# A gated recurrence over 512 steps: the columns of its three PSUM banks regrouped to 192, 128 and 64

## The chip, the cores and the metric

The kernel runs on one core of one Trainium2 chip. The metric is the device time in microseconds (us) of one launch; the time before is the median of three runs.

## The reference

Eight sequences (batch B = 8) of T = 512 steps with 512 features go through a gated recurrent cell with 512 units, and the cell's output is added to its input. All arithmetic is float32.

```python
def step(h, x_t):
    fused = jax.nn.sigmoid(jnp.concatenate([x_t, h], axis=-1) @ w_W + w_b)
    hidden_state, output_state = jnp.split(fused, 2, axis=-1)          # r, z
    memory_state = x_t @ wx_W + wx_b + hidden_state * (h @ wh_W + wh_b)
    h_new = output_state * h + (1.0 - output_state) * jnp.tanh(memory_state)
    return (h_new, h_new)
_, hs = jax.lax.scan(step, h0, jnp.swapaxes(x, 0, 1))
out = x + jnp.swapaxes(hs, 0, 1)
```

In the kernel's names, r is the gate on the hidden product, z the gate that keeps the old state, hh the product h @ wh_W with its bias, and x the product x_t @ wx_W with its bias. Every step needs the state of the step before.

## The kernel before

**Layout.** The state is kept with units on partitions, in four tiles of 128 units, k = 0 to 3. Half A is k = 0 and 1 (tiles `hTA`), half B is k = 2 and 3 (`hTB`). A matmul takes the state as the loaded weights (128 partitions, 32 columns: four steps of eight sequences, of which the rows of the current step are filled and the others are zero) and streams weight columns against it. Its output lies on 32 PSUM partitions. Index j = 0 to 3 names the four such strips, each with its own 128 of the 512 units, so that one (bank, k) is four matmuls, one for each strip. The strips can run side by side on TensorE. Each float32 matmul appears in the trace as two records.

**Banks.** Four steps make a group, g. Each group has three PSUM banks of 128 columns, in two sets for even and odd groups: R holds r of both halves, G holds hh and z of half A, H holds z and hh of half B. ScalarE first copies the x-side products into a bank (`spread`, L248 at the copy), and the matmuls of the steps then accumulate onto them.

**One step on TensorE.** The order is written out: `ORDER = "R0 R1 G0 G1 R2 R3 G2 G3 H0 H1 H2 H3"`, four matmuls for each word, 48 in all, so R0 needs the first tile of the new state and R2 the third. After them come seven matmuls of 192 columns for the x-side of a later group (`products`, tiles `xp`), from step 5 on until the last ten steps, for which none are left. The strip at which a step starts is turned by seven each time, so that the three spare places rotate. All matmuls go through one helper and have line L188.

**One step on VectorE and ScalarE.** VectorE takes the sums back to units-on-partitions by 32x32 transposes, and does the gating by scans (`tensor_tensor_scan`: multiply by one operand, add the other), one for each k. ScalarE does the sigmoids and the tanh. All its activations have line L216.

- `turn_r(hf)`: transpose of r into `tr` (L377), sigmoid into `md0`.
- `turn_h(hf)`: transpose of hh into `md1` (L395).
- `turn_z(hf)`: transpose of z into `tz` (L377), sigmoid of the negative into `hd0`. Its transpose is made to wait for the sigmoid of r by a manual dependency.
- `memory(hf)`: two scans `m` from `md0` and `md1` (L357), each followed by a tanh on ScalarE into a slot of the state tile.
- `update(hf)`: two scans from `hd0` and the state tile into the next state tile (L357), one for each k.

The order of these calls is the order on both engines:

```python
turn_r(0); turn_r(1); turn_h(0); turn_z(0); memory(0); update(0)
turn_h(1); turn_z(1); memory(1); update(1)
```

After that follow, in each step, two copies of the new state into another slot (ScalarE), one transpose of an x-side block for the next group (`turn_x`, L252), in some steps copies and sums for the x-side, three tiny memsets (L497), and two additions of input and state on GpSimd (L499) into the output tile. VectorE, ScalarE and GpSimd each work in the order written.

**Loads.** SP loads the weights at the start (`wx`, `wgr`, `whh`) and then one chunk of 16 steps of x at a time, and stores the output by chunks.

Of the kernel before, what the change touches and what calls it, by code (L numbers as in the profile page):

```python
# [7 lines left out]
F32 = mybir.dt.float32  # L8
BF16 = mybir.dt.bfloat16
AF = mybir.ActivationFunctionType  # L10
ALU = mybir.AluOpType
PSUM = bass.MemoryType.PSUM

P = 128
NQ = 4
GS = 4
B = 8
HU = 64
# [5 lines left out]
LAST = 4  # L24
SYNC = mybir.DependencyInfo(mybir.DependencyClass.Sync, mybir.DependencyReason.DATA)

ORDER = "R0 R1 G0 G1 R2 R3 G2 G3 H0 H1 H2 H3"

FIRST = "Q0 x Q1 x Q2 x Q3 H0 H1 H2 H3"

BANKS = ("R", "G", "H")

HALF = 192

AL, BE = (0, slice(64, 256)), (0, slice(256, 448))
GA, DE = (1, slice(64, 256)), (1, slice(256, 448))

XP = {"G": slice(0, 128), "R": slice(128, 256), "X": slice(256, 384), "H": slice(384, 512)}


@with_exitstack
def tile_cond_rnn_residual(
# [2 lines left out]
    x: bass.AP,  # L45
    xh: bass.AP,
    wx_d: bass.AP,
    wgr_d: bass.AP,
    whh_d: bass.AP,
    wh3_d: bass.AP,  # L50
    bias_d: bass.AP,
    out: bass.AP,
    TC: int,
# [28 lines left out]
    nc = tc.nc  # L82
    NCH = x.shape[0]
    T = NCH * TC
    NG = T // GS

    const = ctx.enter_context(tc.tile_pool(name="const", bufs=1))
    xin_p = ctx.enter_context(tc.tile_pool(name="xin", bufs=4))
    out_p = ctx.enter_context(tc.tile_pool(name="outp", bufs=3))
    work = ctx.enter_context(tc.tile_pool(name="work", bufs=4))  # L90
    psum = ctx.enter_context(tc.tile_pool(name="psum", bufs=1, space=PSUM))
# [31 lines left out]
    wx = const.tile([P, NQ, NQ, 384], F32, name="wx")  # L123
    for k in range(NQ):
        nc.sync.dma_start(out=wx[:, k], in_=wx_d[k])

    wgr = const.tile([P, NQ, NQ, 256], F32, name="wgr")
    for k in range(NQ):
        nc.sync.dma_start(out=wgr[:, k], in_=wgr_d[k])
    whh = const.tile([P, NQ, NQ, 128], F32, name="whh")  # L130
    nc.sync.dma_start(out=whh[:, :3], in_=whh_d)
    nc.sync.dma_start(out=whh[:, 3], in_=wh3_d)

    def wh(bank, k, j):
        return whh[:, k, j] if bank == "H" else wgr[:, k, j, {"G": slice(0, 128), "R": slice(128, 256), "Q": slice(0, 256)}[bank]]

    load_x(0, 1)

# [6 lines left out]
    NH = 2 * GS  # L145
# [29 lines left out]
    def state(hf, i, slot=2):  # L175

        s = i % GS
        return hT[hf][i % NH][:, B * s : B * s + B, :, slot]

    ctx.enter_context(tc.manual_schedule())  # L180
    banks = [
        {n: psum.tile([P, 128], F32, name=f"{n}{q}") for n in BANKS}
        for q in range(2)
    ]
    xps = [psum.tile([P, 512], F32, name=f"xp{q}") for q in range(2)]
# [1 line left out]
    def mm(out_, lhsT, rhs, start=False):  # L187
        nc.tensor.matmul(  # L188
            out_, lhsT, rhs, start=start, stop=False, skip_group_check=True
        )  # L190


    for t_ in list(banks[0].values()) + list(banks[1].values()):
        mm(t_, none[:, :128], none, start=True)
    def warm():

        mm(xps[1], zeros[:, :128], zeros)
# [17 lines left out]
    def act(key, out_, in_, func, **kw):  # L215
        inst = nc.scalar.activation(out_, in_, func, **kw).ins  # L216
        if key in written:
            tc.declare_no_dep(inst, written[key], reason="ordered through VectorE")
        written[key] = inst
        return inst  # L220
# [17 lines left out]
    def late(g):  # L238

        if g == 0:  # L240
            return xps[0][:, 256:512]
        return even if g % 2 == 0 else odd[g // 2 % 2]

    def spread(g, names):

        for n in names:
            src = late(g)[:, 128:256] if n == "H" else xps[g % 2][:, XP[n]]
            nc.scalar.copy(banks[g % 2][n], src)  # L248

    def turn_x(g, e):  # L250

        nc.vector.transpose(  # L252
            md1[e // 2][g % 2][:, :, e % 2, 1], late(g)[:, 32 * e : 32 * e + 32]
        )

    def reg(r):
        return xps[r[0]][:, r[1]]
# [61 lines left out]
    first = {g: prefill(g) for g in (1, 2, 3)}  # L319
    weight_sum(0)  # L320
    weight_sum(2)
    spread(0, "RGH")
    for e in range(NQ):
        turn_x(0, e)

    pool_done = {}
    for i in range(T):
# [7 lines left out]

        for n in (ORDER if i else FIRST).split():
            if n == "x":
                take(first[1], 1)
                continue
            bank, k = n[0], int(n[1])  # L340
            hs = hT[k // 2][i % NH][:, :, k % 2, 2]
            for j in range(NQ):
                j = (j + turn[0]) % NQ
                to = xps[0][:, :256] if bank == "Q" else ps[bank]
                mm(to[32 * j : 32 * j + 32, :], hs, wh(bank, k, j))
        if i < 5:
            take(first[(i + 3) // 2], 2)
# [3 lines left out]

        rows = slice(B * s, B * s + B)

        def scans(hf, out_, d0, d1):

            for c_ in (slice(0, 1), slice(1, 2)):
                nc.vector.tensor_tensor_scan(  # L357
                    *[t_[:, :, c_].rearrange("p n c s -> p (n c s)") for t_ in (out_, d0, d1)],
                    0.0,
                    ALU.mult,  # L360
                    ALU.add,
                )
                yield c_

        if i:
            pg, pr = ps["G"], ps["R"]
        else:
            pg, pr = (xps[0][:, XP[n]] for n in "GR")
        raw = {
            "h": (pg[:, :HU], ps["H"][:, HU:]),  # L370
            "z": (pg[:, HU:], ps["H"][:, :HU]),
            "r": (pr[:, :HU], pr[:, HU:]),
        }

        def turned(n, hf):
            t_ = work.tile([P, 2, 32], F32, tag=f"t{n}{hf}", name=f"t{n}{hf}_{i}")
            inst = nc.vector.transpose(t_.rearrange("p c n -> p (c n)"), raw[n][hf]).ins  # L377
            return t_[:, :, rows], inst
# [1 line left out]
        r_done = [None, None]  # L380

        def turn_r(hf):
            tr, inst = turned("r", hf)

            if hf == 1 and i + 1 - NH in pool_done:
                tc.add_manual_dep(inst, pool_done[i + 1 - NH].name, SYNC)
            r_done[hf] = act(
                ("r", hf, g % 2, s),
                md0[hf][g % 2][:, rows, :, 1].rearrange("p n c -> p c n"),
                tr,  # L390
                AF.Sigmoid,
            )

        def turn_h(hf):
            nc.vector.transpose(  # L395
                md1[hf][g % 2][:, :, :, 0].rearrange("p n c -> p c n"), raw["h"][hf]
            )

        def turn_z(hf):
            tz, inst = turned("z", hf)  # L400

            tc.add_manual_dep(inst, r_done[hf].name, SYNC)
            act(
                ("zc", hf, i % 2),
                hd0[hf][i % 2][:, :, :, 2].rearrange("p n c -> p c n"),
                tz,
                AF.Sigmoid,
                scale=-1.0,
            )

        def memory(hf):

            m = work.tile([P, 2, B, 2], F32, tag=f"m{hf}", name=f"m{hf}_{i}").rearrange("p c n s -> p n c s")
            for c_ in scans(hf, m, md0[hf][g % 2][:, rows], md1[hf][g % 2][:, rows]):
                act(("n", hf, c_.start, i % NH), state(hf, i, 1)[:, :, c_], m[:, :, c_, 1], AF.Tanh)

        def update(hf):
            s1 = (i + 1) % GS
            new = hT[hf][(i + 1) % NH][:, B * s1 : B * s1 + B]
            for _ in scans(hf, new, hd0[hf][i % 2], hT[hf][i % NH][:, rows]):  # L420
                pass

        turn_r(0)
        turn_r(1)
        turn_h(0)
        turn_z(0)
        memory(0)
        update(0)
        if i == 0:

            seed(2)
        if i == T - 1:
# [3 lines left out]
                state(0, T),  # L436
                ALU.add,
            )
        turn_h(1)
        turn_z(1)  # L440
        memory(1)
        update(1)
        for hf in range(2):
            act(("h", hf, (i + 1) % NH), state(hf, i + 1, 0), state(hf, i + 1), AF.Copy)
        if i < 3:
# [3 lines left out]
        nxt, two = o + 1 < NG // 2, o + 2 < NG // 2  # L449
        if i == 0:  # L450
            nc.scalar.copy(odd[0], xps[1][:, 256:512])
        if g + 1 < NG:
            turn_x(g + 1, s)
        if i == 0:
            spread(1, "R")
        if u == 0:
            spread(2 * o + 1, "G")
            if o and nxt:
                nc.scalar.copy(reg(GA), reg(BE))
        elif u == 1:  # L460
            spread(2 * o + 1, "H")
        elif u == 2 and o == 0:
            seed(3)
            nc.scalar.copy(even, xps[0][:, 256:512])
        elif u == 2 and nxt:
            last = odd[(o + 1) % 2][:, :HALF]
            nc.vector.tensor_tensor(last, reg(GA), both, ALU.add)
        elif u == 3 and nxt:
            if o:
                nc.vector.tensor_tensor(even[:, :HALF], reg(BE), both, ALU.add)  # L470
            spread(2 * o + 2, "R")
        elif u == 4 and nxt:
            if o == 0:
                nc.scalar.copy(odd[1], xps[1][:, 256:512])
            spread(2 * o + 2, "G")
            if two:
                nc.scalar.copy(reg(AL), bias[:, AL[1]])
                x_sum(o + 2, 0)
        elif u == 5 and nxt:
            spread(2 * o + 2, "H")  # L480
            if two:
                nc.scalar.copy(reg(DE), step_bias)
                x_sum(o + 2, 1)
        elif u == 6 and two:
            nc.scalar.copy(reg(BE), reg(AL))
            x_sum(o + 2, 2)
        elif u == 7 and nxt:
            spread(2 * o + 3, "R")
            if two:
                nc.scalar.copy(both, reg(DE))  # L490
                x_sum(o + 2, 3)
# [104 lines left out]
```

## Time and profile before

| | |
|---|---|
| Time, three runs | 1681.29 us median (1680.15 to 1682.52) |
| Profiled execution, own time | 1682.46 us |
| Its span, first to last instruction | 1679.9 us |
| Granted TensorE clock, mean | 0.999 |
| TensorE matmul busy | 1668.8 us, 99% of the span |
| VectorE busy | 1144.5 us, 68% |
| ScalarE busy | 947.4 us, 56% |
| GpSimd busy | 303.5 us, 18% |
| DMA moved | 31.37 MB, mean 19 GB/s |

The profile is of one execution. Busy shares count time in which at least one instruction of the engine is recorded; matmul records overlap, since they are pipelined. A line of the timeline gives start and duration in us, engine, line, operation, output and inputs with shapes, how many instructions are merged, and in brackets the idle time of the engine before it with what ended that. The view rounds to 10 ns; the trace's records, from which single steps are read, are in ns. "Seen" means that the waiting engine starts, some time after the record of the producer ended.

### The profile page before, as it was taken

How to read it: one execution, taken by the hardware profiler on the slowest of the kernel's cores; microseconds unless marked ns; L12 is line 12 of the kernel's file. 1: busy time of each engine (PE TensorE's matmuls, PEld its weight loads, DVE VectorE, ACT ScalarE, POOL GpSimd, SP SyncE). 2: the span in 40 equal slices, each digit the busy share in tenths (PEclk: the TensorE clock that was granted, in tenths of full speed). 3: DMA queues.
4: the chain of work that ended last, by engine and by line, in shares of the span. 5: the costliest groups of instructions: out<-in, count | busy, mean ns of one | idle time of the engine just before them, and what ended most of it. 6: DMA issues, size and time to landing. Idle time of an engine off the chain costs nothing.

```text
span 1679.9 us, 129621 instructions
## 1 busy us (share of the span) xinstructions
PE 1668.8 (99%) x56206; PEld 1645.4 (98%) x56206; DVE 1144.5 (68%) x9387; ACT 947.4 (56%) x5822; POOL 303.5 (18%) x1281
## 2 busy tenths in 40 slices
PE   8999999999999999999999999999999999999998
PEld 5999999999999999999999999999999999999997
DVE  6766666666666666666666666666666666666666
ACT  3555555555555555555555555555555555555554
POOL 1111111111111111111111111111111111111111
PEclk9999999999999999999999999999999999999999
DMA  4000000000000000000000000000000000000000
GB/s 178 17 5 17 18 18 17 17 5 18 17 18 18 5 17 18 17 17 5 18 18 17 18 15 7 18 17 17 17 5 18 17 18 17 5 18 12 11 11 10
DMA packets 11523, 31.37 MB, mean 19 GB/s; under 512 B 1220, under 2 KB 1732, under 8 KB 10952
## 3 DMA queue, kind: packets, MB, share of 16 engines
q1 hardware_dynamic: 10800, 22.94, 3.9%
q8 instruction: 439, 7.19, 1.7%
q14 instruction: 132, 1.08, 0.2%
q10 hardware_dynamic: 152, 0.16, 0.0%
HBM read 14.70 MB, written 8.39 MB: 14 GB/s over the span
## 4 chain that ended last, share of the span: by engine, by line
PE 99%; DVE 1%; DMA 0%; ACT 0%; issue 0%
PE R L188 27%; PE G L188 26%; PE H L188 26%; PE xp L188 19%; DMA rows<-in_bias_dram 0%; DVE md1A L395 0%; DVE hTA L357 0%; ACT hd0A L216 0%; DVE tz L377 0%; ACT hTA L216 0%; DVE bias L203 0%; DVE rows L120 0%; ACT hTB L216 0%; DVE hTB L357 0%; ACT hd0B L216 0%
## 5 line engine op out<-in xcount | busy, mean ns | idle before, releaser
L188 PE MATMUL R<-wgr,hTA 128*32 128x128 f32 x8176 | 431.5, 275 | 2.4 <-DVE hTA L357 2.2
L188 PE MATMUL G<-wgr,hTA 128*32 128x128 f32 x8176 | 411.9, 273 | 0.0
L377 DVE STREAM_TRANSPOSE tr<-R 128x64 f32<-128x64 f32 x1022 | 194.4, 228 | 286.9 <-PE R L188 286.8
L188 PE MATMUL R<-wgr,hTB 128*32 128x128 f32 x8176 | 385.9, 275 | 0.0
L499 POOL TENSOR_TENSOR ot<-xin,hTB 128x16 f32<-128x16 f32 x503 | 126.6, 252 | 1331.5 <-DVE hTB L357 1323.4
L188 PE MATMUL H<-whh,hTB 128*32 128x128 f32 x8192 | 366.4, 273 | 0.0
L188 PE MATMUL H<-whh,hTA 128*32 128x128 f32 x8192 | 366.2, 273 | 0.0
L188 PE MATMUL G<-wgr,hTB 128*32 128x128 f32 x8176 | 365.5, 273 | 0.0
L188 PEld LDWEIGHTS G<-wgr,hTA 128*32 128x32 f32 x8176 | 334.5, 122 | 0.2
L188 PEld LDWEIGHTS R<-wgr,hTA 128*32 128x32 f32 x8176 | 301.2, 123 | 9.0 <-DVE hTA L357 5.5
L188 PEld LDWEIGHTS H<-whh,hTB 128*32 128x32 f32 x8192 | 289.0, 122 | 0.1
L188 PEld LDWEIGHTS H<-whh,hTA 128*32 128x32 f32 x8192 | 289.0, 122 | 0.1
L188 PEld LDWEIGHTS G<-wgr,hTB 128*32 128x32 f32 x8176 | 288.6, 122 | 0.0
L216 ACT ACTIVATE hd0B<-tz 128x16 f32<-128x16 f32 x512 | 116.5, 228 | 279.4 <-DVE tz L377 279.3
L188 PEld LDWEIGHTS R<-wgr,hTB 128*32 128x32 f32 x8176 | 255.2, 123 | 2.2 <-DVE hTB L357 0.5
L216 ACT ACTIVATE md0A<-tr 128x16 f32<-128x16 f32 x512 | 112.0, 219 | 237.5 <-DVE tr L377 237.4
L188 PE MATMUL xp<-tw,sx 128*32 128x192 f32 x2976 | 229.3, 326 | 0.0
L357 DVE TENSOR_TENSOR_SCAN hTB<-hd0B,hTB 128x24 f32<-128x24 f32 x1024 | 158.0, 196 | 104.6 <-ACT hTB L216 104.4
L357 DVE TENSOR_TENSOR_SCAN hTA<-hd0A,hTA 128x24 f32<-128x24 f32 x1024 | 157.7, 195 | 103.2 <-ACT hTA L216 103.2
L188 PE MATMUL xp<-wx,xin 128*32 128x192 f32 (+1 forms) x2048 | 178.2, 331 | 0.4 <-issue 0.4
L216 ACT ACTIVATE hd0A<-tz 128x16 f32<-128x16 f32 x512 | 115.7, 226 | 111.1 <-DVE tz L377 111.1
L216 ACT ACTIVATE hTB<-hTB 128x16 f32<-128x16 f32 x512 | 120.4, 235 | 79.6 <-DVE hTB L357 70.9
(90 smaller groups left out, 2408.9 us busy)
## 6 DMA issues: line engine op xcount, KB each, us to landing
xin<-in_x_dram SPq DMA_DIRECT2D x31, 256.0 KB, 3.5
out_dram<-ot SPq DMA_DIRECT2D x31, 256.0 KB, 2.2
wx<-in_wx_dram SPq DMA_DIRECT2D x4, 768.0 KB, 7.0
wgr<-in_wgr_dram SPq DMA_DIRECT2D x4, 512.0 KB, 9.7
whh<-in_whh_dram SPq DMA_DIRECT2D x1, 768.0 KB
whh<-in_wh_dram SPq DMA_DIRECT2D x1, 256.0 KB, 10.9
out_dram<-ot SPq DMA_DIRECT2D x1, 192.0 KB, 1.8
head<-in_xh_dram ACTq DMA_DIRECT2D x1, 144.0 KB, 5.0
```

The source lines that it names most:

```text
L188: nc.tensor.matmul(out_, lhsT, rhs, start=start, stop=False, skip_group_check=True)
L216: inst = nc.scalar.activation(out_, in_, func, **kw).ins
L357: nc.vector.tensor_tensor_scan(*[t_[:, :, c_].rearrange("p n c s -> p (n c s)") for t_ in (out_, d0, d1)], 0.0, ALU.mult, ALU.add,)
L377: inst = nc.vector.transpose(t_.rearrange("p c n -> p (c n)"), raw[n][hf]).ins
L499: return engine.tensor_tensor(ot[:, t, 2 * hf : 2 * hf + 2, :].rearrange("p c n -> p n c"), x_of(c, slice(2 * hf, 2 * hf + 2), t, 1).rearr ...
```

## The change

The columns are dealt to the banks anew. Bank A holds hh, z and r of half A (192 columns), bank B holds r and hh of half B (128), bank C holds z of half B (64). The order on TensorE becomes `A0 B0 A1 A2 A3 B1 B2 B3 C0 C1 C2 C3`. On VectorE and ScalarE, r of half B is turned after the memory scans of half A; the two updates of half A are set apart, with turn_r(1) before the first and turn_h(1) and turn_z(1) between them. turn_z(0) keeps its wait for the sigmoid of r; turn_z(1) loses it, and the second update of half A takes it. The wait for GpSimd moves from turn_r(1) to turn_h(0). The x-side tile is laid out to match (192 columns for A, then X, C and B), turn_x runs one step earlier and reads some blocks from PSUM, and the weight tiles are regrouped (`wa` 192 columns, `wb` 192). The number of matmuls, transposes, scans and activations of a step stays the same.

```diff
-ORDER = "R0 R1 G0 G1 R2 R3 G2 G3 H0 H1 H2 H3"
+ORDER = "A0 B0 A1 A2 A3 B1 B2 B3 C0 C1 C2 C3"
-FIRST = "Q0 x Q1 x Q2 x Q3 H0 H1 H2 H3"
+FIRST = "A0 x A1 x A2 x A3 B0 B1 B2 B3 C0 C1 C2 C3"
-BANKS = ("R", "G", "H")
+BANKS = {"A": 192, "B": 128, "C": 64}
...
-XP = {"G": slice(0, 128), "R": slice(128, 256), "X": slice(256, 384), "H": slice(384, 512)}
+XP = {"A": slice(0, 192), "X": slice(192, 320), "C": slice(320, 384), "B": slice(384, 512)}
...
     def wh(bank, k, j):
-        return whh[:, k, j] if bank == "H" else wgr[:, k, j, {"G": slice(0, 128), "R": slice(128, 256), "Q": slice(0, 256)}[bank]]
+        return wa[:, k, j] if bank == "A" else wb[:, k, j, {"C": slice(0, 64), "B": slice(64, 192)}[bank]]
...
     def turn_x(g, e):
-        nc.vector.transpose(
-            md1[e // 2][g % 2][:, :, e % 2, 1], late(g)[:, 32 * e : 32 * e + 32]
-        )
+        c0 = XP["X"].start + 32 * e
+        nc.vector.transpose(md1[e // 2][g % 2][:, :, e % 2, 1], part(g, c0, c0 + 32))
...
         raw = {
-            "h": (pg[:, :HU], ps["H"][:, HU:]),
-            "z": (pg[:, HU:], ps["H"][:, :HU]),
-            "r": (pr[:, :HU], pr[:, HU:]),
+            "h": (pa[:, :HU], ps["B"][:, HU:]),
+            "z": (pa[:, HU : 2 * HU], ps["C"]),
+            "r": (pa[:, 2 * HU :], ps["B"][:, :HU]),
         }
...
         def turn_r(hf):
-            tr, inst = turned("r", hf)
-            if hf == 1 and i + 1 - NH in pool_done:
-                tc.add_manual_dep(inst, pool_done[i + 1 - NH].name, SYNC)
+            tr, _ = turned("r", hf)
...
         def turn_h(hf):
-            nc.vector.transpose(
+            inst = nc.vector.transpose(
                 md1[hf][g % 2][:, :, :, 0].rearrange("p n c -> p c n"), raw["h"][hf]
-            )
+            ).ins
+            if hf == 0 and i + 1 - NH in pool_done:
+                tc.add_manual_dep(inst, pool_done[i + 1 - NH].name, SYNC)
         def turn_z(hf):
             tz, inst = turned("z", hf)
-            tc.add_manual_dep(inst, r_done[hf].name, SYNC)
+            if hf == 0:
+                tc.add_manual_dep(inst, r_done[0].name, SYNC)
...
         turn_r(0)
-        turn_r(1)
         turn_h(0)
         turn_z(0)
-        memory(0)
-        update(0)
+        memory(0, 0)
+        memory(0, 1)
+        turn_r(1)
+        update(0, 0)
+        turn_h(1)
+        turn_z(1)
+        tc.add_manual_dep(update(0, 1), r_done[1].name, SYNC)
...
-        turn_h(1)
-        turn_z(1)
-        memory(1)
-        update(1)
+        memory(1, 0)
+        memory(1, 1)
+        update(1, 0)
+        update(1, 1)
...
-        if g + 1 < NG:
-            turn_x(g + 1, s)
+        ahead = 2 * o + (1 if u < 3 else 2 if u < 7 else 3)
+        if ahead < NG:
+            turn_x(ahead, (u + 1) % GS)
...
-            spread(2 * o + 1, "G")
+            spread(2 * o + 1, "B")
...
-            spread(2 * o + 1, "H")
+            spread(2 * o + 1, "C")
...
-            spread(2 * o + 2, "R")
+            spread(2 * o + 2, "A")
```

Here `memory(hf, q)` and `update(hf, q)` do one of the two scans (and, for memory, its tanh) that `memory(hf)` and `update(hf)` did in a loop.

More of the change, by code (lines that the diff above doesn't have):

```diff
@@ L47, in tile_cond_rnn_residual @@
     wx_d: bass.AP,
-    wgr_d: bass.AP,
-    whh_d: bass.AP,
-    wh3_d: bass.AP,
+    wa_d: bass.AP,
+    wb_d: bass.AP,
+    wb3_d: bass.AP,
     bias_d: bass.AP,
@@ L125, in tile_cond_rnn_residual @@
         nc.sync.dma_start(out=wx[:, k], in_=wx_d[k])
-    wgr = const.tile([P, NQ, NQ, 256], F32, name="wgr")
+    wa = const.tile([P, NQ, NQ, 192], F32, name="wa")
     for k in range(NQ):
[L129 to L132, printed above, removed]
+        nc.sync.dma_start(out=wa[:, k], in_=wa_d[k])
+    wb = const.tile([P, NQ, NQ, 192], F32, name="wb")
+    nc.sync.dma_start(out=wb[:, :3], in_=wb_d)
+    nc.sync.dma_start(out=wb[:, 3], in_=wb3_d)
     def wh(bank, k, j):
-        return whh[:, k, j] if bank == "H" else wgr[:, k, j, {"G": slice(0, 128), "R": slice(128, 256), "Q": slice(0, 256)}[bank]]
+        return wa[:, k, j] if bank == "A" else wb[:, k, j, {"C": slice(0, 64), "B": slice(64, 192)}[bank]]
     load_x(0, 1)
@@ L181, in tile_cond_rnn_residual @@
     banks = [
-        {n: psum.tile([P, 128], F32, name=f"{n}{q}") for n in BANKS}
+        {n: psum.tile([P, w], F32, name=f"{n}{q}") for n, w in BANKS.items()}
         for q in range(2)
@@ L193, in tile_cond_rnn_residual @@
     for t_ in list(banks[0].values()) + list(banks[1].values()):
-        mm(t_, none[:, :128], none, start=True)
+        mm(t_, none, none[:, :1].broadcast_to([P, t_.shape[1]]), start=True)
     def warm():
@@ L242, in late, with part @@
         return even if g % 2 == 0 else odd[g // 2 % 2]
+    def part(g, c0, c1):
+        return late(g)[:, c0 - 256 : c1 - 256] if c0 >= 256 else xps[g % 2][:, c0:c1]
     def spread(g, names):
         for n in names:
-            src = late(g)[:, 128:256] if n == "H" else xps[g % 2][:, XP[n]]
-            nc.scalar.copy(banks[g % 2][n], src)
+            nc.scalar.copy(banks[g % 2][n], part(g, XP[n].start, XP[n].stop))
     def turn_x(g, e):
-        nc.vector.transpose(
-            md1[e // 2][g % 2][:, :, e % 2, 1], late(g)[:, 32 * e : 32 * e + 32]
-        )
+        c0 = XP["X"].start + 32 * e
+        nc.vector.transpose(md1[e // 2][g % 2][:, :, e % 2, 1], part(g, c0, c0 + 32))
     def reg(r):
@@ L321, in tile_cond_rnn_residual @@
     weight_sum(2)
-    spread(0, "RGH")
+    spread(0, "BCA")
     for e in range(NQ):
@@ L343, in tile_cond_rnn_residual @@
                 j = (j + turn[0]) % NQ
-                to = xps[0][:, :256] if bank == "Q" else ps[bank]
+                to = ps[bank] if i or bank != "A" else xps[0][:, XP["A"]]
                 mm(to[32 * j : 32 * j + 32, :], hs, wh(bank, k, j))
@@ L352, in tile_cond_rnn_residual, with scan @@
         rows = slice(B * s, B * s + B)
[L354 to L361, printed above, removed]
-                )
[L363 to L368, printed above, removed]
+        def scan(c_, out_, d0, d1):
+            return nc.vector.tensor_tensor_scan(
+                *[t_[:, :, c_].rearrange("p n c s -> p (n c s)") for t_ in (out_, d0, d1)],
+                0.0,
+                ALU.mult,
+                ALU.add,
+            ).ins
+        pa = ps["A"] if i else xps[0][:, XP["A"]]
         raw = {
-            "h": (pg[:, :HU], ps["H"][:, HU:]),
-            "z": (pg[:, HU:], ps["H"][:, :HU]),
-            "r": (pr[:, :HU], pr[:, HU:]),
+            "h": (pa[:, :HU], ps["B"][:, HU:]),
+            "z": (pa[:, HU : 2 * HU], ps["C"]),
+            "r": (pa[:, 2 * HU :], ps["B"][:, :HU]),
         }
@@ L394, in turn_h @@
         def turn_h(hf):
-            nc.vector.transpose(
+            inst = nc.vector.transpose(
                 md1[hf][g % 2][:, :, :, 0].rearrange("p n c -> p c n"), raw["h"][hf]
-            )
+            ).ins
+            if hf == 0 and i + 1 - NH in pool_done:
+                tc.add_manual_dep(inst, pool_done[i + 1 - NH].name, SYNC)
         def turn_z(hf):
             tz, inst = turned("z", hf)
-            tc.add_manual_dep(inst, r_done[hf].name, SYNC)
+            if hf == 0:
+                tc.add_manual_dep(inst, r_done[0].name, SYNC)
             act(
@@ L409, in turn_z, with memory, update @@
             )
[L411 to L417, printed above, removed]
+        ms = [
+            work.tile([P, 2, B, 2], F32, tag=f"m{hf}", name=f"m{hf}_{i}").rearrange("p c n s -> p n c s")
+            for hf in range(2)
+        ]
+        def memory(hf, q):
+            c_ = slice(q, q + 1)
+            scan(c_, ms[hf], md0[hf][g % 2][:, rows], md1[hf][g % 2][:, rows])
+            act(("n", hf, q, i % NH), state(hf, i, 1)[:, :, c_], ms[hf][:, :, c_, 1], AF.Tanh)
+        def update(hf, q):
             s1 = (i + 1) % GS
             new = hT[hf][(i + 1) % NH][:, B * s1 : B * s1 + B]
-            for _ in scans(hf, new, hd0[hf][i % 2], hT[hf][i % NH][:, rows]):
-                pass
+            return scan(slice(q, q + 1), new, hd0[hf][i % 2], hT[hf][i % NH][:, rows])
         turn_r(0)
-        turn_r(1)
         turn_h(0)
         turn_z(0)
-        memory(0)
-        update(0)
+        memory(0, 0)
[5 more added lines that the diff above has]
+        tc.add_manual_dep(update(0, 1), r_done[1].name, SYNC)
         if i == 0:
@@ L451, in tile_cond_rnn_residual @@
             nc.scalar.copy(odd[0], xps[1][:, 256:512])
-        if g + 1 < NG:
-            turn_x(g + 1, s)
-        if i == 0:
-            spread(1, "R")
+            spread(1, "A")
+            turn_x(1, 0)
+        ahead = 2 * o + (1 if u < 3 else 2 if u < 7 else 3)
+        if ahead < NG:
+            turn_x(ahead, (u + 1) % GS)
         if u == 0:
-            spread(2 * o + 1, "G")
+            spread(2 * o + 1, "B")
             if o and nxt:
@@ L474, in tile_cond_rnn_residual @@
                 nc.scalar.copy(odd[1], xps[1][:, 256:512])
-            spread(2 * o + 2, "G")
+            spread(2 * o + 2, "B")
             if two:
@@ L479, in tile_cond_rnn_residual @@
         elif u == 5 and nxt:
-            spread(2 * o + 2, "H")
+            spread(2 * o + 2, "C")
             if two:
@@ L487, in tile_cond_rnn_residual @@
         elif u == 7 and nxt:
-            spread(2 * o + 3, "R")
+            spread(2 * o + 3, "A")
             if two:
@@ L551 @@
     w, wxm, whm = f["L0_cond_w_W"], f["L0_cond_wx_W"], f["L0_cond_wh_W"]
-    wb, wxb, whb = f["L0_cond_w_b"], f["L0_cond_wx_b"], f["L0_cond_wh_b"]
+    wb_, wxb, whb = f["L0_cond_w_b"], f["L0_cond_wx_b"], f["L0_cond_wh_b"]
     def quads(a):
@@ L565, in chunks @@
         return c_(units(a).swapaxes(0, 1))
-    wx_d = chunks(cat((z[:D], half_a), (r[:D], both), (wxm, both), (z[:D], half_b)))
-    wgr_d = chunks(cat((whm, half_a), (z[D:], half_a), (r[D:], both)))
-    wh = units(cat((z[D:], half_b), (whm, half_b)))
-    whh_d, wh3_d = c_(wh[:, :3]), c_(wh[:, 3])
-    rb, zb = wb[:512], wb[512:]
-    bias_d = c_(cat((whb, half_a), (zb, half_a), (rb, both), (wxb, both), (zb, half_b), (whb, half_b))[0])
+    wx_d = chunks(cat((z[:D], half_a), (r[:D], half_a), (wxm, both), (z[:D], half_b), (r[:D], half_b)))
+    wa_d = chunks(cat((whm, half_a), (z[D:], half_a), (r[D:], half_a)))
+    wb = units(cat((z[D:], half_b), (r[D:], half_b), (whm, half_b)))
+    wb_d, wb3_d = c_(wb[:, :3]), c_(wb[:, 3])
+    rb, zb = wb_[:512], wb_[512:]
+    bias_d = c_(
+        cat((whb, half_a), (zb, half_a), (rb, half_a), (wxb, both), (zb, half_b), (rb, half_b), (whb, half_b))[0]
+    )
     xd = units(_np.moveaxis(x, 2, 0))
@@ L582 @@
     for name, a in (
-        ("x", xd), ("xh", xh_d), ("wx", wx_d), ("wgr", wgr_d), ("whh", whh_d), ("wh3", wh3_d), ("bias", bias_d),
+        ("x", xd), ("xh", xh_d), ("wx", wx_d), ("wa", wa_d), ("wb", wb_d), ("wb3", wb3_d), ("bias", bias_d),
     ):
```

## The prediction

> **What bounds the kernel now.** I read the page first (busy time, then the chain that ended last), then the costliest groups by form, then the timeline of single steps.
>
> ```profile
> PE 1668.8 (99%) x56206; PEld 1645.4 (98%) x56206; DVE 1144.5 (68%) x9387; ACT 947.4 (56%) x5822; POOL 303.5 (18%) x1281
> PE 99%; DVE 1%; DMA 0%; ACT 0%; issue 0%
> ```
>
> By these lines TensorE is everything. But a matmul's record is several times longer than its stream, so overlapping records hide gaps. The four column strips (j = 0..3) work side by side, each on its own queue. Within a strip, starts lie 109 ns apart at 128 columns, 163 at 192 and 216 at 256, at a granted clock of 1.00; every fp32 matmul is two such passes. Call one pass of all four strips a round. A step has 24 rounds of 128, 24 x 109 = 2616 ns, and seven x-side matmuls of 192 columns, 14 passes over four strips, 3.5 x 163 = 571 on average: 3187 ns. Three strips carry four x passes (3268 ns), the fourth only two. The mean step, weight load of R0 to the next, takes 3240. So about 50 ns a step are waiting. The timeline shows where:
>
> ```profile
> 800.15 0.31 DVE L357 TENSOR_TENSOR_SCAN hTA<-hd0A,hTA 128x24 f32<-128x24 f32 x2 [0.20 <-ACT hTA L216]
> 800.41 0.31 PE L188 MATMUL R<-wgr,hTA 128*32 128x128 f32 x1
> 801.12 0.31 DVE L357 TENSOR_TENSOR_SCAN hTB<-hd0B,hTB 128x24 f32<-128x24 f32 x2 [0.21 <-ACT hTB L216]
> 801.38 0.31 PE L188 MATMUL R<-wgr,hTB 128*32 128x128 f32 x1
> ```
>
> Both matmuls last 312 ns instead of 273: 40 ns pass between their weight load and their start. The loads start 54 ns after the end of the first scan of hTA and of hTB (5th to 95th percentile over all steps 53 to 55). R0 and R2 wait for the state in every step: the kernel is a ring of TensorE, VectorE and ScalarE, closed twice a step. The last steps, which have no x-side, show the ring bare:
>
> ```profile
> 1650.51 0.31 DVE L357 TENSOR_TENSOR_SCAN hTA<-hd0A,hTA 128x24 f32<-128x24 f32 x2 [0.20 <-ACT hTA L216]
> 1650.77 0.66 PE L188 MATMUL R<-wgr,hTA 128*32 128x128 f32 x16 [0.22 <-DVE hTA L357]
> 1651.47 0.31 DVE L357 TENSOR_TENSOR_SCAN hTB<-hd0B,hTB 128x24 f32<-128x24 f32 x2 [0.20 <-ACT hTB L216]
> 1651.73 0.66 PE L188 MATMUL R<-wgr,hTB 128*32 128x128 f32 x16
> 1652.21 0.62 PE L188 MATMUL G<-wgr,hTB 128*32 128x128 f32 x16
> 1652.90 0.25 DVE L395 STREAM_TRANSPOSE md1A<-G 128x64 f32<-128x64 f32 x1
> 1653.07 0.21 DVE L377 STREAM_TRANSPOSE tz<-G 128x64 f32<-128x64 f32 x1
> 1653.31 0.22 ACT L216 ACTIVATE hd0A<-tz 128x16 f32<-128x16 f32 x1 [0.21 <-DVE tz L377]
> 1653.43 0.30 ACT L216 ACTIVATE hTA<-m 128x8 f32<-128x8 f32 x2
> 1653.66 0.31 DVE L357 TENSOR_TENSOR_SCAN hTA<-hd0A,hTA 128x24 f32<-128x24 f32 x2 [0.20 <-ACT hTA L216]
> 1653.93 0.33 PE L188 MATMUL R<-wgr,hTA 128*32 128x128 f32 x4 [0.22 <-DVE hTA L357]
> ```
>
> In ns: load of R0 to load of R2 965; to the last G matmul's start 828 (40 load, 20 stagger of the strips, 7 x 109); 272 its record, 66 until VectorE starts on G; 1029 from there to the next load of R0 (174 transpose of h, 206 of z, 34, 123 to the tanh behind the sigmoid of z, 196 tanh, 32, 208 scan, 54, rounded). Sum 3160; the trace's steps there take 3159. With the x-side the mean is 3240, between this ring and the fuller strips' 3268. Note that r of half A is long done: only z and h wait for G.
>
> **The change, part by part.** *TensorE, columns.* Matmuls per step stay 48 + 7. Rounds become eight each of 192, 128 and 64 columns. The line through 109, 163 and 216 gives 56 for 64 columns (estimate): 8 x (163 + 109 + 56) = 2624, 8 ns more than 2616. No matmul of before is narrower than 128. Bounds for the 64-column round: below, 56, since nothing in the line allows less; above, 109, the narrowest round seen. I take 56: at 1650.77 four strips load weights 7 ns apart and each starts 40 ns after its load, so neither load nor issue fills 56 ns.
>
> The Trainium skill (TensorE: Matmul & The Clock Gate, "Wait — 56ns, not 53.3ns?") speaks against this: starts of matmuls never come closer than about 25 ns, however narrow. Taken over four strips that would make a round 100 ns, the step's stream 3187 + 8 + 8 x 44 = 3547, and the time about 1834 us. The row above has starts 7 ns apart on different strips, so I read the rule as one strip's, where 56 is above it.
>
> *Half A's chain.* Now r, h and z of half A all come from bank A. R2's place is taken by A2; behind its load lie only four rounds of 192: 40 + 20 + 3 x 163 = 549 to the last start, 279 less than 828. But r now lies on the path: turn_r, its sigmoid, and turn_z(0), which waits for that sigmoid (the built program lists it as waiting for ScalarE). The first step, where r, h and z of half A come together, shows this sequence already:
>
> ```profile
> 19.08 0.38 DVE L377 STREAM_TRANSPOSE tr<-xp 128x64 f32<-128x64 f32 x2 [4.04 <-PE xp L188]
> 19.61 0.25 DVE L377 STREAM_TRANSPOSE tz<-xp 128x64 f32<-128x64 f32 x1
> 19.79 0.23 DVE L357 TENSOR_TENSOR_SCAN m<-md0A,md1A 128x16 f32<-128x16 f32 x2
> ```
>
> From tr to tz 536 (251 transpose, 34, 218 sigmoid, 33 back); tz 250, since a transpose that has waited takes longer than the 206 of one that follows on. Then 34, 123, 196, 32, 208, 54 as before: 1433 against 1029, 404 more. Queued behind the waiting tz: scan m, turn_r(1), the updates. The wait for A's end: 326 (192-column record) + 66.
>
> *Half B's chain.* From update(0,0) to update(1,0): 125, turn_h 148, turn_z 131, update(0,1) 102, scan m 172, 34, tanh 198, 32 = 942, against 965; the sigmoid of z ends its slot earlier (125 + 148 + 207 + 34 + 123 = 637, against 712 where the tanh gets its input). Its new waits are covered, counted from where VectorE sees A: bank B is seen at 655 and turn_r(1) is reached at 897; bank C is seen at 1103 and turn_z(1) is reached at 1444. That cover of 341 ns is gone if the 64-column round exceeds 56 by 43. update(0,1), now behind turn_h(1) and turn_z(1), feeds A1 381 ns after A0's load; A0 and B0 fill 544.
>
> *Hidden or neutral.* turn_x is one 128x32 transpose a step as before (188 ns), two of four from PSUM, after the scans of hTB, where VectorE then idles hundreds of ns before bank A. The spreads copy the same 384 columns, behind the state copies on ScalarE. GpSimd's wait moves from turn_r(1) to turn_h(0), eight steps old: nothing. SP issues the same weight bytes in as many transfers; I allow 0.5 us either way at the start and take 0.
>
> **Sum.** New ring: 942 + 549 + 326 + 66 + 1433 = 3316. Fuller strips stream 2624 + 652 = 3276, less than the ring, so the ring sets every step. Steps with x-side: 496 x (3316 - 3240) = 37.7 us. Last nine: 9 x (3316 - 3159) = 1.4. The profiled execution took 1682.46 (span 1679.9 and 2.6 around it): 1721.6; it lies 1.2 above the median 1681.29, so 1720.
>
> The ring's uncertain terms: tz 206 (44 less) and the 38 ns from a matmul's end to VectorE seen in most x-side steps (28 less) give 3244; the fuller strips then share the limit, halfway 3260: 1693. Other transposes and scans that wait anew could each cost 20 to 45 more: ring 3370, 1746.
>
> **Rivals.** *A floor under 64 columns.* At 109 a round the mean stream is 3187 + 8 + 8 x 53 = 3619: 496 x 379 = 188 us, 1869. For: no narrow row. Against: the 40 ns load and 7 ns starts. It decides above 61 ns a round, where fuller strips pass 3316.
>
> *Faster: the wait of tz is void.* If turn_z(0) ran straight behind turn_h(0) while r's sigmoid works, scan m would start at 535 and the tanh at 743: chain 743 + 196 + 32 + 208 + 54 = 1233, ring 3116, 43 under 3159. The short strip would wait 43 less, a quarter of it per step: 11 ns x 496 = 5.3, less 0.4 at the end, 1676. It decides once the ring is below 3159, that is 157 ns under my sum. For: the earlier end of A (279 - 54 = 225 ns) is real. Against: the row at 19.61 and the wait in the built program.
>
> *It doesn't bite.* Were the strips alone the limit in both, 8 ns x 496 = 4 us at most, or nothing. Against: 54 ns after the scan in every step.
>
> **Numbers.** Ring 0.78; floor 0.12; void wait 0.07; no bite 0.03. The measurement can tell about 0.2% (3.4 us) from no change. The range 1693 to 1746 takes in the ring's bounds and a floor up to some 68 ns. Slower 0.90, same 0.03, faster 0.07.
>
> **What would show it.** Right: tz of half A starts some 535 ns after its tr in every step, TensorE's load of A0 54 ns after the scan of hTA, even steps of about 3316 with and without x-side, VectorE idle before tz. Floor: starts on bank C 100 ns apart and C the last wait of tz<-C. Wrong: tz right behind md1A, or steps under 3240.

## The result, and the profile after

The changed kernel takes 1721.39 us (median of four runs, 1720.66 to 1721.63), against 1681.9 us for the kernel before on the same chip. The ratio is 1.0234, 95% interval 1.0216 to 1.0252: slower, by about 39 us. The prediction was 1720, range 1693 to 1746. The profiled execution of the changed kernel took 1721.52 us, with a span of 1719.1 and a granted clock of 1.000.

From the page of the changed kernel, the busy times, the chain that ended last and two of the costliest groups (busy us, mean ns of one, idle before and what ended it):

```profile
PE 1706.4 (99%) x56238; PEld 1453.2 (85%) x56238; DVE 1126.2 (66%) x9387; ACT 957.2 (56%) x5822; POOL 303.1 (18%) x1281
PE 98%; DVE 1%; ACT 0%; DMA 0%; issue 0%
...
L188 PE MATMUL C<-wb,hTA 128*32 128x64 f32 x8192 | 208.4, 219 | 0.0
L374 DVE STREAM_TRANSPOSE tz<-A 128x64 f32<-128x64 f32 x511 | 128.0, 250 | 78.9 <-ACT md0A L216 73.7
```

Matmul still shows 99% and 98% of the chain, as before, though the kernel now waits in every step. What moved is the weight load: 85% busy where it was 98%. (The Trainium skill, Perfetto Trace Analysis, "Identifying the Most-Contended Engine", calls matmul busy time a poor measure of headroom and names the busy share of weight loads as a better one; this pair of profiles agrees, 99% twice against 98% and 85%.) The tz group shows the other half: its mean is 250 ns, the duration of a transpose that has waited, and it waits for the sigmoid of r. The waits of the changed kernel (us in total, times, longest) say how often:

```profile
DVE tr L374 <- PE A L188: 357.4, 510, 1.0
PEld A L188 <- DVE hTB L358: 93.5, 505, 0.6
DVE tz L374 <- ACT md0A L216: 73.7, 476, 0.2
```

TensorE's loads wait for the scan of hTB in 505 steps. In the same view of the kernel before, R0's loads waited visibly for the state 11 times, 5.5 us in all (R2's twice, 0.5 us):

```profile
PEld R L188 <- DVE hTA L357: 5.5, 11, 0.7
```

One step from the timeline of the changed kernel, with x-side:

```profile
799.89 0.87 PE L188 MATMUL A<-wa,hTB 128*32 128x192 f32 x16
800.83 0.25 DVE L374 STREAM_TRANSPOSE tr<-A 128x64 f32<-128x64 f32 x1 [0.53 <-PE A L188]
801.00 0.21 DVE L389 STREAM_TRANSPOSE md1A<-A 128x64 f32<-128x64 f32 x1
801.12 0.22 ACT L216 ACTIVATE md0A<-tr 128x16 f32<-128x16 f32 x1 [0.91 <-DVE tr L374]
801.24 0.41 PE L188 MATMUL C<-wb,hTA 128*32 128x64 f32 x16
801.37 0.25 DVE L374 STREAM_TRANSPOSE tz<-A 128x64 f32<-128x64 f32 x1
801.46 0.41 PE L188 MATMUL C<-wb,hTB 128*32 128x64 f32 x16
801.54 0.24 DVE L358 TENSOR_TENSOR_SCAN m<-md0A,md1A 128x16 f32<-128x16 f32 x2
801.77 0.30 ACT L216 ACTIVATE hTA<-m 128x8 f32<-128x8 f32 x2
802.00 0.21 DVE L358 TENSOR_TENSOR_SCAN hTA<-hd0A,hTA 128x24 f32<-128x24 f32 x1
802.93 0.31 DVE L358 TENSOR_TENSOR_SCAN hTB<-hd0B,hTB 128x24 f32<-128x24 f32 x2 [0.19 <-ACT hTB L216]
803.19 0.35 PEld L188 LDWEIGHTS A<-wa,hTB 128*32 128x32 f32 x12 [0.18 <-DVE hTB L358]
```

This is the ring in one view: A2's load at 799.89, A's end at 800.76, tr at 800.83, tz half a microsecond later at 801.37 when md0A is done, the scan of hTA at 802.00, the scan of hTB 0.93 later, and A2's load again at 803.19, 3.30 us after the last. The four 64-column rounds of C0 and C1 start between 801.24 and 801.46: 55 ns a round.

Where the 39 us come from, from the starts of the hTA scans in the two profiles: the 492 steps from the tenth to the 502nd take 3308 ns instead of 3235 (35.9 us); the last nine, without x-side, 3304 instead of 3158 (1.3); the first ten, 57.6 us instead of 55.6 (2.0).

### The profile page after: what moved, and what is told of

The parts are those of the page before. It is cut to its first block, busy times and chain, and to the rows that moved or that the text cites. A ratio compares the mean times of both kernels' runs of the same rounds, so it can differ in the third digit from the quotient of the medians.

```text
span 1719.1 us, 129875 instructions
## 1 busy us (share of the span) xinstructions
PE 1706.4 (99%) x56238; PEld 1453.2 (85%) x56238; DVE 1126.2 (66%) x9387; ACT 957.2 (56%) x5822; POOL 303.1 (18%) x1281
## 4 chain that ended last, share of the span: by engine, by line
PE 98%; DVE 1%; ACT 0%; DMA 0%; issue 0%
PE A L188 40%; PE B L188 26%; PE xp L188 20%; PE C L188 13%; DMA rows<-in_bias_dram 0%; DVE tz L374 0%; DVE tr L374 0%; ACT md0A L216 0%; ACT hd0A L216 0%; DVE hTA L358 0%; ACT hTA L216 0%; DVE bias L203 0%; ACT hTB L216 0%; ACT xp L224 0%; DVE rows L120 0%
## 5 line engine op out<-in xcount | busy, mean ns | idle before, releaser
L188 PE MATMUL A<-wa,hTA 128*32 128x192 f32 x8176 | 558.6, 329 | 4.0 <-DVE hTA L358 4.0
L188 PE MATMUL A<-wa,hTB 128*32 128x192 f32 x8176 | 446.4, 336 | 0.2 <-DVE hTB L358 0.2
L188 PE MATMUL B<-wb,hTA 128*32 128x128 f32 x8192 | 421.0, 273 | 0.0
L188 PEld LDWEIGHTS A<-wa,hTB 128*32 128x32 f32 x8176 | 242.1, 125 | 113.0 <-DVE hTB L358 93.5
L188 PEld LDWEIGHTS B<-wb,hTA 128*32 128x32 f32 x8192 | 308.5, 122 | 24.2
L188 PE MATMUL B<-wb,hTB 128*32 128x128 f32 x8192 | 317.8, 273 | 0.0
L188 PEld LDWEIGHTS A<-wa,hTA 128*32 128x32 f32 x8176 | 242.6, 123 | 73.6 <-DVE hTA L358 6.0
L188 PEld LDWEIGHTS B<-wb,hTB 128*32 128x32 f32 x8192 | 240.5, 122 | 0.0
L188 PE MATMUL C<-wb,hTA 128*32 128x64 f32 x8192 | 208.4, 219 | 0.0
L188 PE MATMUL C<-wb,hTB 128*32 128x64 f32 x8192 | 208.4, 219 | 0.0
```

The source lines that it names most:

```text
L188: nc.tensor.matmul(out_, lhsT, rhs, start=start, stop=False, skip_group_check=True)
```

## The experiments

Each ratio is to runs of the kernel before on the same chip: 1680.32 us for the first four, 1683.62 for the next four, 1680.98 for the last.

**tz without its wait.** The changed kernel with the manual dependency of turn_z(0) taken out.

```diff
         def turn_z(hf):
             tz, inst = turned("z", hf)
-            if hf == 0:
-                tc.add_manual_dep(inst, r_done[0].name, SYNC)
```

> The changed kernel, but the transpose of z of half A no longer waits for the sigmoid of r; the scan m waits for it instead. Theory (the ring, with r's sigmoid and tz in series on it): 200 ns leave half A's chain (1433 to 1233), ring 3308 - 200 = 3108, or some 3170 if the double wait of m costs VectorE one more semaphore instruction; steps again share the limit with the strips, 3222 to 3240 ns: 1675 to 1685 us, no longer slower than before. Rival (the wider bank A and the order of the matmuls cost the time, the wait is hidden): stays above 1715 us.

Measured: 1681.07 us, ratio 1.0006 (0.9996 to 1.0015). VectorE in two of its last steps:

```profile
1651.59 0.25 DVE L374 STREAM_TRANSPOSE tr<-A 128x64 f32<-128x64 f32 x1 [0.75 <-PE A L188]
1651.89 0.21 DVE L374 STREAM_TRANSPOSE tz<-A 128x64 f32<-128x64 f32 x1
1652.12 0.28 DVE L358 TENSOR_TENSOR_SCAN m<-md0A,md1A 128x16 f32<-128x16 f32 x2
1652.59 0.21 DVE L358 TENSOR_TENSOR_SCAN hTA<-hd0A,hTA 128x24 f32<-128x24 f32 x1
1654.73 0.25 DVE L374 STREAM_TRANSPOSE tr<-A 128x64 f32<-128x64 f32 x1 [0.76 <-PE A L188]
```

tz now follows at 0.30 us, the scan of hTA comes 1.00 us after tr instead of 1.17, and tr comes again after 3.14 us instead of 3.30. The whole loss is gone with this one wait; whatever else the regrouping costs does not show in the time. The bare ring is 164 ns shorter and not the expected 200 (3140 instead of 3108): from the start of the first scan m to the tanh 225 ns pass where 208 were counted on, since that scan now waits itself and takes 192 ns, and from the tanh to the scan of hTA 246 instead of 228.

**r on the path in the old banks.** The kernel before, its banks untouched, with r's matmuls exchanged with G's so that tr has to wait for the later of the two.

```diff
-ORDER = "R0 R1 G0 G1 R2 R3 G2 G3 H0 H1 H2 H3"
+ORDER = "G0 G1 R0 R1 G2 G3 R2 R3 H0 H1 H2 H3"
```

> The kernel before, banks and VectorE order unchanged, but the matmuls of G ahead of those of R, so that r of half A comes last. Theory (r on half A's path is what costs): tr to tz 536 ns, chain 1433 instead of 1029, ring 967 + 828 + 338 + 1433 = 3566, steps even near 3560, 1846 us. Rival (the loss of the change comes from its bank widths): within 10 us of 1682.

Measured: 1850.38 us, ratio 1.1009 (1.0992 to 1.1025), some 4 us above the expected 1846; even steps of 3564. VectorE:

```profile
1652.05 0.38 DVE L377 STREAM_TRANSPOSE tr<-R 128x64 f32<-128x64 f32 x2 [0.98 <-PE R L188]
1652.59 0.25 DVE L377 STREAM_TRANSPOSE tz<-G 128x64 f32<-128x64 f32 x1
1655.62 0.38 DVE L377 STREAM_TRANSPOSE tr<-R 128x64 f32<-128x64 f32 x2 [0.75 <-PE R L188]
```

The same 0.54 us from tr to tz as in the changed kernel, in banks of 128 columns. The bare ring is 3561 against 3159: r on the path costs 402 ns, where the prediction's arithmetic has 404.

**C2 and C3 left out** of the changed kernel, to see whether TensorE's load bounds it.

```diff
-ORDER = "A0 B0 A1 A2 A3 B1 B2 B3 C0 C1 C2 C3"
+ORDER = "A0 B0 A1 A2 A3 B1 B2 B3 C0 C1"
```

> The changed kernel without the matmuls C2 and C3 (z of half B lacks half of its product with the state): four rounds of 64 columns less per step, 220 ns of TensorE. Theory (the ring sets the step, and bank C is not on it): 1721 us, within 3. Rival (TensorE, 99% busy, sets the time): 512 x 220 ns less, 1609 us.

Measured: 1717.2 us, ratio 1.0218 (1.0203 to 1.0233), steps of 3305 instead of 3308. A seventh of the 56 thousand matmul records is gone and the steps stay: TensorE's stream is not the bound. The time lies 1 us under the expected band; most of that is the start, where the tenth update came at 54.8 us instead of 57.6.

**H2 and H3 left out** of the kernel before, the same question there.

```diff
-ORDER = "R0 R1 G0 G1 R2 R3 G2 G3 H0 H1 H2 H3"
+ORDER = "R0 R1 G0 G1 R2 R3 G2 G3 H0 H1"
```

> The kernel before without the matmuls H2 and H3 (z and hh of half B lack half of their product with the state): four rounds of 128 less, 436 ns a step. Theory (before stood between a ring of 3159 and strips of 3268): strips 2832, ring alone, 3159 in all steps, 1682 - 38 = 1644 us. Rival 1 (TensorE sets the time): 1682 - 223 = 1459. Rival 2 (ring alone, strips without part in it): 1682.

Measured: 1642.56 us, ratio 0.9776 (0.976 to 0.9793), every step 3159. From its waits:

```profile
PEld R L188 <- DVE hTA L357: 204.0, 511, 0.9
```

Freed of a few rounds, the loads wait for hTA in all 511 steps and the steps are the bare ring, neither the shorter stream (2751) nor the old 3235. So the kernel before was bounded by both: a ring of 3159 and strips of 3268, with TensorE's load adding 76 ns a step. This is why a ring that grew by 145 (3304 - 3159) made the x-side steps only 73 longer.

**The changed kernel again**, beside the next three.

> The changed kernel itself, so that the next three are compared on one chip. 1720 us, within 3; the first scan of hTA stood at 21.5 us in its first profile and at 19.4 in two kernels with the same loads, so some 2 us of the start may belong to that run.

Measured: 1721.15 us, ratio 1.0221 (1.0207 to 1.0235).

**The updates together again.** The changed kernel with the old order of half A's updates and of half B's transposes.

```diff
         update(0, 0)
+        update(0, 1)
         turn_h(1)
         turn_z(1)
-        tc.add_manual_dep(update(0, 1), r_done[1].name, SYNC)
```

The wait of update(0,1) goes back to turn_z(1) with it.

> The changed kernel with the two updates of half A together again, ahead of turn_h(1) and turn_z(1). Theory (from update(0,0) to update(1,0) is the second arc of the ring): 967 ns as before instead of the measured 931, ring 3308 + 36 = 3344, 18 us more than the changed kernel: 1738. Rival (half B's state is early enough, only half A's chain counts): no change, 1720.

Measured: 1738.82 us, ratio 1.0326 (1.031 to 1.0342), 17.7 over the run beside it. VectorE:

```profile
1651.94 0.31 DVE L358 TENSOR_TENSOR_SCAN hTA<-hd0A,hTA 128x24 f32<-128x24 f32 x2
1652.91 0.31 DVE L358 TENSOR_TENSOR_SCAN hTB<-hd0B,hTB 128x24 f32<-128x24 f32 x2 [0.19 <-ACT hTB L216]
```

The scans of hTA and hTB are 0.97 us apart instead of 0.93, and the step is 3345. The order of the updates is a gain inside the change, worth 37 ns of ring here.

**The updates apart, alone.** The kernel before with that part only, and with G0 ahead of R1 so that TensorE has work while the second tile is late.

```diff
-ORDER = "R0 R1 G0 G1 R2 R3 G2 G3 H0 H1 H2 H3"
+ORDER = "R0 G0 R1 G1 R2 R3 G2 G3 H0 H1 H2 H3"
...
-        update(0)
+        up = update(0)
+        next(up)
+        turn_h(1)
+        turn_z(1)
+        take(up)
...
-        turn_h(1)
-        turn_z(1)
         memory(1)
-        update(1)
+        take(update(1))
```

Here `update` yields after each of its two scans.

> The kernel before with this part of the change alone: the first update of half A, turn_h(1), turn_z(1), then its second update; TensorE order R0 G0 R1 G1 for the later second tile. Theory: 967 becomes 931, bare ring 3159 - 36 = 3123 in the last nine steps; the other steps share the limit with the strips, and take 2 ns (as from 3159 to 3140 in the run without tz's wait) to 9 ns (a quarter of 36) less: 1 to 5 us under before. Rival (the strips alone limit): no change in the steps with x-side.

Measured: 1680.98 us, ratio 0.9982 (0.9973 to 0.999), a bare ring of 3132 where 3123 was expected: from the scan of hTA to that of hTB 938 ns pass, not 931. The time is 2.6 us under the kernel before, within the expected 1 to 5. But the profile does not show the steps with x-side any shorter: their mean is 3236 against 3235 in the profile of the kernel before, and 15 of them are more than 110 ns above the median, 4.9 us together. So the rival is not excluded, and where the 2.6 us come from is open.

**The shortest ring.** The changed kernel without tz's wait, and with turn_h(1) ahead of the first update.

```diff
         turn_r(1)
-        update(0, 0)
         turn_h(1)
+        update(0, 0)
         turn_z(1)
```

> The changed kernel without tz's wait, and with turn_h(1) ahead of the first update, in the time in which VectorE waits for the tanh (bank B is seen at 655, the update starts at 1008). Theory: 148 leave the way from update(0,0) to update(1,0), 932 - 148 = 784, so that A2 no longer waits (A0, B0, A1 stream 870); ring then 60 + 1359 to A's last start, 392, 1270 = 3081 instead of 3140; strips with only one wait left: steps of 3195 (mean stream) to 3225, 1661 to 1676 us, under both kernels. Rival (the strips' uneven load is all that is left): as without it, 1681.

Measured: 1680.56 us, ratio 0.9977 (0.9968 to 0.9986): 3 us under the kernel before on its chip, but some 5 us above the expected band, and as a number the rival's 1681. The bare ring came out as expected. VectorE in the last steps:

```profile
1642.24 0.25 DVE L374 STREAM_TRANSPOSE tr<-A 128x64 f32<-128x64 f32 x1 [0.92 <-PE A L188]
1643.25 0.20 DVE L358 TENSOR_TENSOR_SCAN hTA<-hd0A,hTA 128x24 f32<-128x24 f32 x1
1644.05 0.31 DVE L358 TENSOR_TENSOR_SCAN hTB<-hd0B,hTB 128x24 f32<-128x24 f32 x2 [0.19 <-ACT hTB L216]
1645.32 0.25 DVE L374 STREAM_TRANSPOSE tr<-A 128x64 f32<-128x64 f32 x1 [0.83 <-PE A L188]
```

hTA to hTB is down to 0.80 us, tr to tr 3.08. The median of the 492 steps with x-side is 3216, within the expected 3195 to 3225, against 3245 in the run with tz free; their mean is 3234 in both. For 34 of them are more than 110 ns above the median, 10.1 us together; the kernel before has 7 such steps, 2.0 us, the run with tz free 13, 3.4 us. In 21 of the 34 TensorE's weight loads pause for 138 to 858 ns (from the start of one load to the start of the next), waiting for nothing that the profile shows ("issue"). One of the pauses, 676 ns from start to start:

```profile
339.91 0.11 PEld L188 LDWEIGHTS xp<-tw,sx 128*32 128x32 f32 x1
340.58 0.12 PEld L188 LDWEIGHTS xp<-tw,sx 128*32 128x32 f32 x3 [0.56 <-issue]
```

**The same with less code.** The trace's DMA records hold a clue. Queue q8 carries instructions in packets of 16,384 bytes: 440 in this run, 376 in the run without C2 and C3, so one for about 256 records of TensorE. Take all pauses of over 250 ns ahead of loads that don't open a step, between the tenth update and the 502nd: 13 in this run, 16 with the updates apart, 7 in the repeat of the changed kernel (none in its first profile, so the number is not fixed by the kernel), 5 with tz free, 2 with the updates together, 1 in the kernel before. All 44 end 1.2 to 1.6 us after a packet of q8 has landed, though packets come only every 3.75 to 3.9 us. So do the pauses of all 21 long steps above (1.24 to 1.54 us). The place in the code agrees: when TensorE's loads, matmul passes and semaphore instructions are numbered in order, each of the 44, and of the 21, stands at number 193 or 194 of a run of 256.

```diff
-ORDER = "A0 B0 A1 A2 A3 B1 B2 B3 C0 C1 C2 C3"
+ORDER = "A0 B0 A1 A2 A3 B1 B2 B3 C0 C1"
```

> As the run with turn_h(1) ahead (1680.56 us; steps 3216 ns in the median, but 34 of the 492 steps from the tenth update on over 110 ns longer than that, 10 us together), with the matmuls C2 and C3 left out, so that z of half B lacks half of its sum. The instruction queue q8 brought 439 or 440 packets in every kernel with all its matmuls, one every 3.73 to 3.87 us, and each of these kernels but one has at least five steps that long; 376 packets, one every 4.2 to 4.4 us, in the two kernels with a sixth of the matmuls of a step left out, and none of these long steps. Theory of late code: at 188 records a step and steps of about 3080 ns the packets come every 4.2 us, so no step is over 110 ns above the median; the ring of 3080 ns sets the steps, since the fuller strips now stream 2400 + 652 = 3052: 1680.6 - 492 x (3.2335 - 3.080) = 1605 us, within 4. Rival, the long steps come from this order of VectorE's work, not from the code: they stay, some 30 of them, and the time is about 1615.

Measured: 1606.99 us, ratio 0.9563 (0.9547 to 0.9579), steps of 3080 in the median; a packet of q8 every 4.2 us. The pauses of TensorE are all gone, and the long steps that they made. But 13 long steps stay, 3.1 us, and so the expectation that none would be left was wrong. They are of a second kind: VectorE is late between tr and the scan of hTA, as in these lines of its timeline, where 0.33 us pass idle:

```profile
781.09 0.21 DVE L374 STREAM_TRANSPOSE tz<-A 128x64 f32<-128x64 f32 x1
781.63 0.28 DVE L358 TENSOR_TENSOR_SCAN m<-md0A,md1A 128x16 f32<-128x16 f32 x2 [0.33 <-ACT hd0A L216]
```

The run before this one has its other 13 long steps there too (3.3 us), and they are the same steps by number, mostly 20 apart (205, 225, 245, 265): their place in the program fixes them. Numbered in the same way, the late instruction of VectorE is number 63 of a run of 128 in all 13; the second queue of instructions, q14, brings packets of 8,192 bytes, half of q8's. So both kinds stand at a fixed place of blocks of code, TensorE's of 256 instructions and VectorE's of 128.

Of the 10 us of long steps in the run before, about 7 go with the blocks of TensorE and vanish where code is needed more slowly. Leaving C2 and C3 out lightens the strips as well, but the run with r on the path in the old banks, which keeps all its matmuls, needs a packet every 4.1 us and has neither such a pause nor a long step; the expectation above, with 3.73 to 3.87 us for every kernel with all its matmuls, overlooks it. That a packet comes too late is not shown: before each pause ended, the last packet had been there for over 1.2 us. (The Trainium skill, Runtime: NRT & Kernel Launch, "Instruction fetch mechanics", says that a long program is streamed in 16 KiB blocks and that the cost of passing from one to the next is mostly hidden. TensorE's blocks here are of that size, VectorE's of half of it; hidden the passing is in most steps, and not in the 44 pauses.)

## Why the prediction was right

*What bounds the kernel before.* Right: a ring of 3159 behind strips of 3268, shown by leaving out H2 and H3. The mean step was taken as 3240, which counted some start-up steps; from the tenth update on it is 3235.

*The new ring.* Term by term, in ns: half B's arc 931 (predicted 942), load to last start of A 549 (549), A's record 326 (326), the way to VectorE 68 (66), half A's arc 1435 (1433). The scan of hTA comes 1173 after tr, predicted 1171. The sum is 3309, and the steps measure 3308 with and 3304 without x-side, against 3316. The only term off by more than 2 ns is half B's arc, where the chain of single durations, 125 + 148 + 131 + 102 + 172, was 11 too long. (The parts given for the old ring's 828, 40 + 20 + 7 x 109, make only 823; the 828 itself is what the trace shows.)

*The pieces also add up, three from runs and one from the traces.* The bare ring before 3159; r on the path +402; A finished earlier, (828 + 272) - (549 + 326) = 225 less; updates set apart 37 less: 3299, measured 3304. With the 27 that setting them apart gave in the old banks it is 3309.

*The sum in time.* Two small errors cancelled. The step grew by 73 instead of 76, 1.8 us less in 492 steps; the start, taken at nothing, cost 2.0 in this profile. In the repeat's profile the start took 55.75 us, hardly more than before, but 5 steps were long (1.5 us): the start is not the change's. And the median lies 0.1 below its own profiled execution, not 1.2 as the kernel before did; that is the last microsecond between 1720 and 1721.4. The ends of the range were not worked out quite as the sum was: by the sum's own terms, steps of 3260 and 3370 give 1692 and 1748 instead of 1693 and 1746, which decides nothing here.

*The covers.* Both held: neither bank B nor bank C ends a wait of VectorE in the waits of the changed kernel, and tz of half B starts 1445 after tr, right where VectorE's order puts it (predicted 1444).

*The rivals.* The floor under 64 columns did not come: 16 passes start in 0.22 us, one every 14 ns over the four strips and one every 55 in a strip (56 predicted). So the skill's floor of about 25 ns holds here, if at all, for one strip, as the prediction read it. The void wait is excluded by the profile after, where tz waits for the sigmoid of r 476 times, and the run with tz free shows what it would have given: 1681, not 1676, since its ring is 3140, not 3116. Its half A's arc took 1268 instead of 1233 (scan m to tanh 225 instead of 208, tanh to the scan of hTA 246 instead of 228), half B's 931 instead of 942. That the change does not bite is excluded by the 39 us themselves, where that rival had 4 at most, and by the run without C2 and C3.

## What to carry to other kernels

When every engine works in a ring, follow one operand around it before regrouping work: here r's sigmoid had been off the path because its bank was finished earlier, and putting r, h and z into one bank brought 400 ns of transpose, sigmoid and hand-overs back for 225 gained by finishing early. Some 164 of the 400 went with one wait put by hand, kept from the old order: look at such waits again when the order changes. The busy share of matmul told nothing of this, at 99% in both kernels; how often weight loads wait for the state did. And the step before, bounded by two limits at once, showed only half of the ring's growth (73 of 145 ns), so size each limit with a run that takes the other away.

## What the runs showed of the hardware

- A transpose of 128x64 out of PSUM took 250 ns after a wait and 206 following on. The first of two scans m took 192 ns instead of 149 when it had to wait itself, and the second then started 109 ns behind it instead of 69.
- TensorE paused for 0.26 to 0.9 us, from one weight load to the next, in a few of 492 steps, always at the same place of a run of 256 of its instructions and 1.2 to 1.6 us after an instruction packet had landed: 1 such pause in the kernel before, none and 7 in two profiles of the changed kernel, up to 16 in other variants, none where a packet was needed only every 4.1 us or more.
- VectorE started late, in 13 steps of the two variants with the shortest ring, 3 us in all, each time at number 63 of a run of 128 of its instructions. Why either engine is late at these places is open.
